# A macaron block with an S4 layer in the middle: the S4 matrix read from DRAM with each partition moved by one value, and the first rows normalized by ScalarE and turned through accumulator banks

## The chip, the core and the metric

The kernel runs on one core of one Trainium2 chip. The metric is the device time of one execution in microseconds (us), taken as the median of several runs. Lower is better. The engines are named as in the profile: PE (TensorE matmul), PEld (its weight loads), DVE (VectorE), ACT (ScalarE), POOL (GpSimd) and SP (SyncE, which issues most DMAs here).

## The reference, cut to what matters

```python
x = L0_attn_u                                   # (2, 1024, 1024) float32
x = x + 0.5 * ffn(layernorm(x))                 # 4-bit weights, HID 1024, INTER 2752
x = x + s4(layernorm(x))
x = x + 0.5 * ffn(layernorm(x))

def ffn(x):                                     # W = scales * (w4 - (z4 + 1)), groups of 128 rows
    return (silu(x @ Wg) * (x @ Wu)) @ Wd

def s4(u):
    Omega = exp(-2j * pi * arange(L) / L)       # L = 1024
    # k00, k01, k10, k11: sums over 64 poles at 1024 points of the circle
    at_roots = c * (k00 - k01 * (1 / (1 + k11)) * k10)
    K = ifft(at_roots, L).real                  # 1024 values, the same for every row
    y = irfft(rfft(u, n=2 * L) * rfft(K, n=2 * L), n=2 * L)[..., :L]
    return y + D[0] * u
```

The last two lines are a causal convolution of each row with K. As a matrix product it needs a Toeplitz matrix: entry (p, c) is K[c - p] for c >= p and 0 before that.

## The kernel before, in words

The 2048 rows are four blocks b of 512 rows (`TB`), each of four tiles t of 128 rows. Eight jobs run in the order `JOBS = [(0, 1), (1, 1), (0, 3), (1, 3), (2, 1), (3, 1), (2, 3), (3, 3)]`: block b and feed-forward k, where k is 1 for the one before S4 and 3 for the one after.

A job has two stages. `gate_up` goes through 64 steps (eight waves of up to three column tiles, times eight row groups of 128). A step loads one weight tile (L456, three steps ahead), multiplies each column tile by the low and the high part of the transposed rows (two PE passes, L496) and then rescales the accumulator in PSUM by the ratio of two groups' scales, on ACT (L472) for the even units and on DVE (L474) for the odd ones. `down` has 44 steps with the same pattern (L555 and again L472 and L474). Job 0 also turns the 4-bit weights into values: DVE subtracts zero points (L395 and L425), SP writes the result to DRAM (`wq`, `wdq`), and all jobs read it from there.

All other work is hung on these steps as hooks (`at(up, step, f)`). The framework then orders the instructions of each engine once, when the program is built; each engine runs its queue in that order and waits on semaphores. So the order on an engine is neither that of the source nor free at run time.

The rows reach PE as follows. `moments` (bn_stats on DVE) and `deviations` (a reciprocal root by three Newton steps, twelve tiny instructions on POOL, L156 to L159) give mean m and reciprocal deviation r. `normalized` (L166) writes (x - m) * r on DVE. `turn` transposes half a tile by four PE transposes into a PSUM bank (L173), ACT copies it as the high part `xTh` (L187), and DVE takes the difference as the low part `xTl` (L188). The banks for this come from the pool `ps` (`bank`), which has two buffers. The accumulators come from the pool `acc`, which has six. For the first block this stands ahead of job 0, the moments in two pairs of tiles, and the dequantization of wave 0 (eight L395) stands between.

The S4 matrix is built once, in the gate_up stage of job 1, by four hooks: `s4_poles` at step 6 (a reciprocal over 128x1024 on DVE, L642), `s4_roots` at step 11, `s4_columns` at step 16 and `s4_toeplitz` at step 22. `s4_roots` takes the sums over poles with eight small matmuls (L681), makes the values at the roots with some 30 DVE instructions of 8 columns, and forms 64 sums of eight products with a table (L727 to L730). `s4_columns` spreads them with 48 DVE instructions of 128x128 (L752 to L754) into the left factors of a product, and `s4_toeplitz` multiplies these with the Fourier tables (16 matmuls of 128x128, two passes each, L764), copies the result on ACT with its columns re-ordered (L771), cuts the lower triangle on POOL (L775) and adds D on the diagonal (L786). The matrix is first read by `convolve` (L797), hung on step 34 of job 1.

Of the kernel before, what the change touches and what calls it, by code (L numbers as in the profile page):

```python
# [9 lines left out]
F32 = mybir.dt.float32  # L10
# [4 lines left out]
AF = mybir.ActivationFunctionType  # L15
ALU = mybir.AluOpType
# [4 lines left out]
P = 128  # L21
# [28 lines left out]
def macaron_s4_kernel(  # L50
# [47 lines left out]
    def bank(name):  # L98
        return ppool.tile([P, 512], F32, tag="ps", name=name)
# [4 lines left out]
    def t4(name):  # L104
        return xpool.tile([P, HID], F32, tag="x", name=name)
# [44 lines left out]
    def deviations(b, k, first=0, eng=None):  # L150

        eng = eng or nc.gpsimd
        mv, ve, r, own = ln.pop((b, first))
        e = small.tile([P, NT], F32, tag="e", name=f"e_{b}_{k}_{first}")[:, own]
        for _ in range(3):
            eng.tensor_tensor(e, r[:, own], r[:, own], ALU.mult)  # L156
            eng.tensor_tensor(e, e, ve, ALU.mult)
            eng.tensor_scalar(e, e, -0.5, 1.5, ALU.mult, ALU.add)
            eng.tensor_tensor(r[:, own], r[:, own], e, ALU.mult)  # L159
        for t in range(own.start, own.stop):  # L160
            ln[b, t] = (mv[:, t, 0:1], r[:, t : t + 1], k)
# [4 lines left out]
        nc.vector.tensor_scalar(n, x[b][t], m, r, ALU.subtract, ALU.mult)  # L166
        return n

    def turned(n, half, name):

        ps = bank(name)
        for k in range(4):
            nc.tensor.transpose(ps[:, bass.ts(k, P)], n[:, bass.ts(4 * half + k, P)], ident)  # L173
        return ps.rearrange("p (c t) -> p c t", c=4)
# [1 line left out]

    pieces = {}

    def turn(b, t, n, half):
        k = ln[b, t][2]  # L180
        if b not in pieces:
            pieces[b] = [
                xtpool.tile([P, NC, TB], F32R, tag="xT", name=f"xT{w}_{b}_{k}") for w in ("h", "l")
            ]
        hi, lo = (a[:, 4 * half : 4 * half + 4, bass.ts(t, P)] for a in pieces[b])
        ps = turned(n, half, f"pt_{b}_{k}_{t}_{half}")
        nc.scalar.copy(hi, ps)  # L187
        nc.vector.tensor_tensor(lo, ps, hi.bitcast(F32), ALU.subtract)  # L188

# [391 lines left out]


    toeplitz = const.tile([P, HID], F32, tag="toeplitz", name="toeplitz")
    s4 = {}

    def s4_poles():
# [88 lines left out]
    def s4_roots():  # L675

        ps = bank("s4_sums")
        for c in range(NC):  # L680
            nc.tensor.matmul(  # L681
                ps[:, 8 * c : 8 * c + 8],
                s4["poles"][:, bass.ts(c, P)],
                s4["weights"],
                start=True,
                stop=True,
            )
        sums = const.tile([P, NC, 8], F32, tag="s4_sums", name="s4_sums_sb")
        nc.vector.tensor_copy(sums.rearrange("p c k -> p (c k)"), ps[:, : 8 * NC])
        half = const.tile([P, 2, NC], F32, tag="s4_half", name="s4_half")  # L690
        nc.sync.dma_start(half, c_half)
        eight = t4("s4_eight").rearrange("p (i n) -> p i n", i=2)
        nc.sync.dma_start(eight, c_eight.partition_broadcast(P))
        hc, hs = half[:, 0, :], half[:, 1, :]

        a = {k: sums[:, :, i] for i, k in enumerate(("00r", "00i", "01r", "01i", "10r", "10i", "11r", "11i"))}
        tmp = {}

        def op(o, l, r, f):
            if o not in tmp:  # L700
                tmp[o] = const.tile([P, NC], F32, tag=f"s4_{o}", name=f"s4_{o}")
            nc.vector.tensor_tensor(tmp[o], l, r, f)
            return tmp[o]

        mul, add, sub = ALU.mult, ALU.add, ALU.subtract
        pr = op("pr", op("m0", a["01r"], a["10r"], mul), op("m1", a["01i"], a["10i"], mul), sub)
        pi = op("pi", op("m0", a["01r"], a["10i"], mul), op("m1", a["01i"], a["10r"], mul), add)
        dr = op("dr", hc, a["11r"], mul)
        nc.vector.tensor_scalar(dr, dr, 1.0, None, add)
        di = op("di", hc, a["11i"], mul)  # L710
        sc = op("sc", op("m0", dr, dr, mul), op("m1", di, di, mul), add)
        nc.vector.reciprocal(sc, sc)
        sc = op("sc", sc, hc, mul)
        nr = op("nr", op("m0", pr, dr, mul), op("m1", pi, di, mul), add)
        ni = op("ni", op("m0", pi, dr, mul), op("m1", pr, di, mul), sub)
        rr = op("qr", a["00r"], op("nr", nr, sc, mul), sub)
        ri = op("qi", a["00i"], op("ni", ni, sc, mul), sub)
        fr = op("fr", op("m0", hc, rr, mul), op("m1", hs, ri, mul), sub)
        fi = op("fi", op("m0", hc, ri, mul), op("m1", hs, rr, mul), add)

        ec, es = (eight[:, i, :].rearrange("p (g c) -> p g c", c=NC) for i in range(2))
        wide = lambda v: v.unsqueeze(1).to_broadcast([P, 64, NC])
        prod = t4("s4_prod").rearrange("p (i n) -> p i n", i=2)
        m0, m1 = (prod[:, i, :].rearrange("p (g c) -> p g c", c=NC) for i in range(2))
        se = const.tile([P, 2, 64], F32, tag="s4_se", name="s4_se")
        for i, (x0, x1, f) in enumerate(((fr, fi, sub), (fi, fr, add))):
            nc.vector.tensor_tensor(m0, ec, wide(x0), mul)  # L727
            nc.vector.tensor_tensor(m1, es, wide(x1), mul)
            nc.vector.tensor_tensor(m0, m0, m1, f)
            nc.vector.tensor_reduce(se[:, i, :], m0, AX.X, add)  # L730
        s4["se"] = se

    def s4_columns():

        cos, sin = t4("s4_tc"), t4("s4_ts")
        nc.sync.dma_start(cos, c_dft[:, 0, :])
        nc.sync.dma_start(sin, c_dft[:, 1, :])
        se = s4["se"]  # L740
        left = [t4("s4_lr"), t4("s4_li")]
        m1 = t4("s4_lm")
        for b in range(8):
            four = lambda ap: ap.rearrange("p (u v) -> p u v", v=8)
            s = [
                se[:, i, 8 * b : 8 * b + 8].unsqueeze(1).to_broadcast([P, 16, 8]) for i in range(2)
            ]
            c, n = four(cos[:, :P]), four(sin[:, :P])
            mb = four(m1[:, bass.ts(b, P)])
            for i, (l0, l1, f) in enumerate(((c, n, ALU.add), (n, c, ALU.subtract))):  # L750
                lb = four(left[i][:, bass.ts(b, P)])
                nc.vector.tensor_tensor(lb, s[0], l0, ALU.mult)  # L752
                nc.vector.tensor_tensor(mb, s[1], l1, ALU.mult)
                nc.vector.tensor_tensor(lb, lb, mb, f)  # L754
        s4["left"], s4["table"] = left, (cos, sin)

    def s4_toeplitz():
        dst = toeplitz.rearrange("p (a b) -> p b a", b=8)
        for i in range(2):
            ps = bank(f"s4_k{i}")  # L760
            for k in range(4):
                b = 4 * i + k
                for part in range(2):
                    nc.tensor.matmul(  # L764
                        ps[:, bass.ts(k, P)],
                        s4["left"][part][:, bass.ts(b, P)],
                        s4["table"][part].rearrange("p (a b) -> p b a", b=8)[:, b, :],
                        start=(part == 0),
                        stop=(part == 1),
                    )  # L770
            nc.scalar.mul(  # L771
                dst[:, 4 * i : 4 * i + 4, :], ps.rearrange("p (b a) -> p b a", b=4), 1.0 / HID
            )
        diag = toeplitz[:, :P]
        nc.gpsimd.affine_select(  # L775
            out=diag,
            in_=diag,
            pattern=[[1, P]],
            compare_op=ALU.is_ge,
            fill=0.0,  # L780
            base=0,
            channel_multiplier=-1,
        )
        d = const.tile([P, 1], F32, tag="s4_d", name="s4_d")
        nc.sync.dma_start(d, dskip.partition_broadcast(P))
        nc.vector.scalar_tensor_tensor(diag, ident, d, diag, ALU.mult, ALU.add)  # L786
        s4.clear()

    def convolve(b, t, lhsT, name):

# [30 lines left out]
    def general():  # L821
# [190 lines left out]

        s4_poles()
        s4_roots()
        s4_columns()
        s4_toeplitz()
        for b in range(TOK // TB):
            load_x(b, rows_of(u, b))
# [16 lines left out]
    def fast():  # L1035
        for j, (b, k) in enumerate(JOBS):
# [50 lines left out]
                at(up, 12, scales_down)  # L1087
                first_weights(up, dn, at)
            if j == 1:
                for s, f in ((6, s4_poles), (11, s4_roots), (16, s4_columns), (22, s4_toeplitz)):  # L1090
                    at(up, s, f)
            if j == 2:
                at(up, 30, in_order)
# [34 lines left out]
    scales(0)  # L1128
    split(0)
    fetch_zeros(0)  # L1130
    for t in (0, 2):
        moments(0, 1, t, 2)
        deviations(0, 1, t)
    for i in range(8):
        dequantize(0, i)
    first = []
    for t in range(NT):
        first.append(normalized(0, t))
        turn(0, t, first[t], 0)
    for t in range(NT):  # L1140
        turn(0, t, first[t], 1)
    x.pop(0)
# [87 lines left out]
```

## Time and profile before

| what | value |
|---|---|
| median of 3 runs | 2228.44 us (2224.03 to 2231.82) |
| the profiled execution's own time | 2229.43 us |
| its span, first to last instruction | 2227.6 us, so 1.8 us lie around it |
| mean granted TensorE clock | 0.989 |
| PE busy | 2146.5 us (96%) |
| DVE busy | 1706.3 us (77%) |
| ACT busy | 1447.6 us (65%) |
| POOL busy | 365.4 us (16%) |
| rescaling on ACT, L472 `pg`, 128x512 | 1264 times 662 ns |
| rescaling on DVE, L474 `pg`, 128x512 | 1144 times 696 ns |

The times of an engine's instructions are from one profiled execution. Matmuls overlap, so the duration of one (some 390 ns for 512 columns) is longer than the step from one to the next, and it is that step that counts in a sum.

### The profile page before, as it was taken

Reading aid. Unit: us, or ns where it says so; the run is one execution under the profiler, and the core shown is the slowest. Engines: PE = TensorE matmul, PEld = TensorE weight load, DVE = VectorE, ACT = ScalarE, POOL = GpSimd, SP = SyncE. Lnnn points to the kernel's source line nnn. Section 1 sums busy time; section 2 is a strip of 40 time slices with the busy share of each in tenths; the row PEclk is TensorE's granted clock in tenths of the full one; section 3 lists DMA queues with packets and bytes.
Section 4 is the critical chain, followed back from the end, with each engine's and each line's share of the span. In section 5 each row is a group of like instructions: output and inputs, shape, how many; then the busy total and the mean of one; then the engine's idle time right before and its main releaser. Section 6 shows DMA issues by size and latency. Waiting matters only on the chain.

```text
span 2227.6 us, 28109 instructions
## 1 busy us (share of the span) xinstructions
PE 2146.5 (96%) x9392; PEld 1690.0 (76%) x9392; DVE 1706.3 (77%) x2705; ACT 1447.6 (65%) x2228; POOL 365.4 (16%) x502
## 2 busy tenths in 40 slices
PE   6998899999999999999999999999999999999998
PEld 4776676767877777888788878777788777888876
DVE  7888779857786878877877777867788677777776
ACT  3777775536764576677767777646776467767775
POOL 1233003212011230122102320102201023012210
PEclk7999999999999999999999999999999999999999
DMA  7888764325443545644455444434444354554444
GB/s 242 284 267 280 251 219 128 121 85 159 135 149 107 174 134 170 225 144 137 143 177 190 130 137 137 148 104 157 138 135 147 107 177 137 153 188 147 134 136 129
DMA packets 161441, 359.86 MB, mean 162 GB/s; under 512 B 20183, under 2 KB 25344, under 8 KB 161290
## 3 DMA queue, kind: packets, MB, share of 16 engines
q1 hardware_dynamic: 160662, 357.64, 50.8%
q8 instruction: 78, 1.28, 0.2%
q14 instruction: 73, 0.60, 0.1%
q10 hardware_dynamic: 628, 0.34, 0.1%
HBM read 307.18 MB, written 50.72 MB: 161 GB/s over the span
## 4 chain that ended last, share of the span: by engine, by line
PE 50%; issue 34%; POOL 7%; DVE 5%; DMA 3%; ACT 0%; SPq 0%; POOLq 0%; DVEq 0%; ACTq 0%
PE pg L496 25%; PE po L555 17%; PE pc L797 5%; POOL hl L523 3%; POOL hh L521 2%; DMA wd<-wdq 1%; DMA w<-wq 1%; DVE pg L474 1%; PE pt L173 1%; PE pb L576 1%; DVE po L474 1%; PE st L173 1%; DVE hf L519 0%; DVE q L395 0%; DMA wdq<-qd 0%
## 5 line engine op out<-in xcount | busy, mean ns | idle before, releaser
L472 ACT ACTIVATE pg<-pg,rat 128x512 f32<-128x512 f32 x1264 | 823.7, 662 | 464.4 <-PE pg L496 461.1
L496 PE MATMUL pg<-xTl,w 128*128 128x512 f32 x2752 | 1088.2, 397 | 33.1 <-DVE pg L474 18.3
L496 PE MATMUL pg<-xTh,w 128*128 128x512 f32 x2752 | 1071.3, 392 | 0.0
L474 DVE TENSOR_TENSOR pg<-pg,rat 128x512 f32<-128x512 f32 x1144 | 780.1, 696 | 168.4 <-PE pg L496 159.6
L496 PEld LDWEIGHTS pg<-xTl,w 128*128 128x128 f32 x2752 | 518.4, 189 | 172.9 <-DVE pg L474 33.5
L496 PEld LDWEIGHTS pg<-xTh,w 128*128 128x128 f32 x2752 | 519.3, 189 | 102.6
L555 PE MATMUL po<-hl,wd 128*128 128x512 f32 x1344 | 538.2, 403 | 14.1 <-DVE po L474 9.2
L472 ACT ACTIVATE po<-po,ratd 128x512 f32<-128x512 f32 x670 | 437.8, 662 | 168.5 <-PE po L555 167.8
L555 PE MATMUL po<-hh,wd 128*128 128x512 f32 x1344 | 521.0, 392 | 0.0
L474 DVE TENSOR_TENSOR po<-po,ratd 128x512 f32<-128x512 f32 x610 | 419.0, 697 | 93.0 <-PE po L555 88.7
L555 PEld LDWEIGHTS po<-hl,wd 128*128 128x128 f32 x1344 | 251.8, 188 | 92.5 <-DVE po L474 21.4
L521 POOL CAST hh<-hf 128x512 fp32r<-128x512 f32 x168 | 109.9, 654 | 1220.1 <-DVE hf L519 1190.2
L555 PEld LDWEIGHTS po<-hh,wd 128*128 128x128 f32 x1344 | 253.3, 188 | 46.2
L523 POOL TENSOR_TENSOR hl<-hf,hh 128x512 fp32r<-128x512 f32 x168 | 221.7, 1320 | 13.3
L519 DVE SCALAR_TENSOR_TENSOR hf<-pg,rat,g 128x512 f32<-128x512 f32 x168 | 125.6, 749 | 80.1 <-ACT g L516 27.9
L516 ACT ACTIVATE g<-pg,rat 128x512 f32<-128x512 f32 x168 | 115.8, 689 | 44.6 <-PE pg L496 41.1
L797 PE MATMUL pc<-toeplitz,st 128*128 128x512 f32 (+3 forms) x384 | 126.5, 486 | 0.0
L797 PEld LDWEIGHTS pc<-toeplitz,st 128*128 128x128 f32 x384 | 70.3, 190 | 57.3 <-issue 46.0
L156 POOL TENSOR_TENSOR e<-r 128x4 f32<-128x4 f32 (+1 forms) x39 | 10.5, 268 | 511.6 <-DVE r L145 509.4
L805 DVE TENSOR_TENSOR x<-x,pc 128x512 f32<-128x512 f32 x32 | 22.0, 687 | 77.6 <-PE pc L797 77.2
L137 DVE BATCH_NORM_STATS2 stats<-x 128x6 f32<-128x512 f32 x96 | 64.6, 680 | 3.2 <-DMA x<-in_L_attn_u_dram 1.9
L187 ACT CAST xTh<-pt 128x512 fp32r<-128x512 f32 x64 | 37.6, 589 | 39.7 <-PE pt L173 39.7
(156 smaller groups left out, 693.0 us busy)
## 6 DMA issues: line engine op xcount, KB each, us to landing
w<-wq SPq DMA_DIRECT2D x320, 384.0 KB
wd<-wdq SPq DMA_DIRECT2D x336, 256.0 KB
w<-wq SPq DMA_DIRECT2D x128, 256.0 KB
w<-wq SPq DMA_DIRECT2D x64, 320.0 KB
x<-in_L_attn_u_dram SPq DMA_DIRECT2D x32, 512.0 KB
wq<-q SPq DMA_DIRECT2D x40, 384.0 KB
wdq<-qd SPq DMA_DIRECT2D x32, 256.0 KB
xs<-x SPq DMA_DIRECT2D x16, 512.0 KB
```

The costliest lines, as they stand in the source:

```text
L137: nc.vector.bn_stats(stats[:, t, i, :], x[b][t][:, bass.ts(i, 512)])
L173: nc.tensor.transpose(ps[:, bass.ts(k, P)], n[:, bass.ts(4 * half + k, P)], ident)
L187: nc.scalar.copy(hi, ps)
L472: nc.scalar.activation(dst, src, AF.Copy, scale=sc)
L474: nc.vector.tensor_tensor(dst, src, sc.to_broadcast([P, TB]), ALU.mult)
L496: nc.tensor.matmul(p, w[:, bass.ts(col, P)], part[:, g, :], start=(g == 0 and k == 0), stop=(g == GK - 1 and k == 1), skip_group_check=True,)
L516: nc.scalar.activation(g, pg, AF.Silu, scale=rat[:, 2 * f, GK - 1 :])
L519: nc.vector.scalar_tensor_tensor(hf, pu, last, g, ALU.mult, ALU.mult)
L521: nc.gpsimd.tensor_copy(hi, hf)
L523: nc.gpsimd.tensor_tensor(lo, hf, hi.bitcast(F32), ALU.subtract)
L555: nc.tensor.matmul(ps[c], w[:, bass.ts(c, P)], part, start=(f == 0 and k == 0), stop=(f == NF - 1), skip_group_check=True,)
L797: nc.tensor.matmul(ps[:, lo - 512 * nh :], lhsT(c), toeplitz[:, lo - P * c : end - P * c], start=(c == 0), stop=(c == last),)
```

## The change: what it does

The change has two parts. In the S4 part, `s4_roots` keeps only 8 of the 64 sums, all its small tiles move into one tile `s4_work`, and a new last DVE instruction turns the sign of the imaginary sums. `s4_columns` is replaced by `s4_response`: 16 matmuls with one moving column each take K from the Fourier tables, DVE scales K and adds D to its first value, and two DMAs write 127 zeros and K to DRAM (`k_dram`). `s4_toeplitz`, now at step 20, reads 128x1024 values back with an access pattern in which each partition starts one value later, and two matmuls with a reversed identity put the partitions in the opposite order. ACT and DVE copy one half each.

In the part for the first rows, the moments of the four tiles are taken together, ACT normalizes in two passes (x - m, then times r), before the dequantization in the source, and the first four halves are turned through the accumulators' pool.

```diff
+    def normalized_on_act(b, t):
+        m, r, k = ln[b, t]
+        n = t4(f"xn_{b}_{k}_{t}")
+        less = small.tile([P, 1], F32, tag=f"less{t}", name=f"less_{t}")
+        nc.gpsimd.tensor_scalar(less, m, -1.0, None, ALU.mult)
+        nc.scalar.activation(n, x[b][t], AF.Identity, bias=less)
+        nc.scalar.activation(n, n, AF.Copy, scale=r)
+        return n
...
-    def turn(b, t, n, half):
+    def turn(b, t, n, half, bank=bank):
...
+    k_dram = dpool.tile([1, P - 1 + HID], F32, tag="k", name="k_dram")
...
-        sums = const.tile([P, NC, 8], F32, tag="s4_sums", name="s4_sums_sb")
+        work = t4("s4_work")
...
-        half = const.tile([P, 2, NC], F32, tag="s4_half", name="s4_half")
+        half = tiny(2 * NC).rearrange("p (i c) -> p i c", i=2)
         nc.sync.dma_start(half, c_half)
...
-        wide = lambda v: v.unsqueeze(1).to_broadcast([P, 64, NC])
+        wide = lambda v: v.unsqueeze(1).to_broadcast([P, 8, NC])
...
+        nc.vector.tensor_scalar(se[:, 1, :], se[:, 1, :], -1.0, None, mul)
         s4["se"] = se
 
-    def s4_columns():
...
-        for b in range(8):
...
-                nc.vector.tensor_tensor(lb, s[0], l0, ALU.mult)
-                nc.vector.tensor_tensor(mb, s[1], l1, ALU.mult)
-                nc.vector.tensor_tensor(lb, lb, mb, f)
+    def s4_response():
+
+        tables = [t4("s4_tc"), t4("s4_ts")]
+        for i in range(2):
+            nc.sync.dma_start(tables[i], c_dft[:, i, :])
+        ps = bank("s4_k")
+        for r in range(8):
+            for i in range(2):
+                nc.tensor.matmul(
+                    ps[:, r : r + 1],
+                    tables[i].rearrange("p (a r) -> p r a", r=8)[:, r, :],
+                    s4["se"][:, i, r : r + 1],
+                    start=(i == 0),
+                    stop=(i == 1),
+                )
+        k = t4("s4_response")
+        d, none = k[:1, 8:9], k[:1, P : 2 * P - 1]
+        nc.sync.dma_start(d, dskip.unsqueeze(0))
+        nc.gpsimd.memset(none, 0.0)
+        nc.vector.tensor_scalar(k[:, :8], ps[:, :8], 1.0 / HID, None, ALU.mult)
+        nc.vector.tensor_tensor(k[:1, 0:1], k[:1, 0:1], d, ALU.add)
+        nc.sync.dma_start(k_dram[:, : P - 1], none)
+        nc.sync.dma_start(k_dram[0, P - 1 :].rearrange("(a r) -> a r", r=8), k[:, :8])
+        s4.clear()
 
     def s4_toeplitz():
...
-        d = const.tile([P, 1], F32, tag="s4_d", name="s4_d")
-        nc.sync.dma_start(d, dskip.partition_broadcast(P))
-        nc.vector.scalar_tensor_tensor(diag, ident, d, diag, ALU.mult, ALU.add)
+        first = k_dram[:]
+        nc.sync.dma_start(rows, bass.AP(first.tensor, first.offset, [[1, P], [1, HID]]))
+        for i in range(NH):
+            ps = bank(f"s4_t{i}")
+            nc.tensor.matmul(ps, turn, rows[:, bass.ts(i, 512)], start=True, stop=True)
+            dst = toeplitz[:, bass.ts(i, 512)]
+            if i:
+                nc.vector.tensor_copy(dst, ps)
+            else:
+                nc.scalar.copy(dst, ps)
...
-                for s, f in ((6, s4_poles), (11, s4_roots), (16, s4_columns), (22, s4_toeplitz)):
+                for s, f in ((6, s4_poles), (11, s4_roots), (16, s4_response), (20, s4_toeplitz)):
...
-    for t in (0, 2):
-        moments(0, 1, t, 2)
-        deviations(0, 1, t)
+    moments(0, 1)
+    deviations(0, 1)
+    first = [normalized_on_act(0, t) for t in range(NT)]
     for i in range(8):
         dequantize(0, i)
-    first = []
     for t in range(NT):
-        first.append(normalized(0, t))
-        turn(0, t, first[t], 0)
+        turn(0, t, first[t], 0, acc)
     for t in range(NT):
         turn(0, t, first[t], 1)
     x.pop(0)
```

## The prediction

> **What bounds the kernel now.** I read the page's busy times first, then its slices.
>
> ```profile
> PE 2146.5 (96%) x9392; PEld 1690.0 (76%) x9392; DVE 1706.3 (77%) x2705; ACT 1447.6 (65%) x2228; POOL 365.4 (16%) x502
> PE   6998899999999999999999999999999999999998
> PEclk7999999999999999999999999999999999999999
> ```
>
> PE bounds it: 81 us of 2227.6 are idle. Only the first slice (55.7 us) shows little PE and a low clock. An engine beside PE can return PE's waits and no more, so the list of PE's waits came next, then the same list for 300 to 460 us, where the S4 matrix is made.
>
> ```profile
> PE pg L496 <- DVE pg L474: 18.3, 22, 3.3
> PE pt L173 <- DVE xn L166: 12.6, 3, 10.4
> ```
>
> ```profile
> PE pg L496 <- DVE pg L474: 1.1, 2, 0.6
> PE pg L496 <- DMA w<-wq: 0.9, 1, 0.9
> ```
>
> (Columns: us in total, times, longest.) The first rows cost PE 12.6 us of waiting before the first product. Around the S4 matrix little is waited for. The timelines of PE, DVE, POOL and SP for the start:
>
> ```profile
> 15.93 0.81 DVE L166 TENSOR_SCALAR xn<-x,mv,r 128x1024 f32<-128x1024 f32 x1 [2.15 <-POOL r L159]
> 17.93 0.94 DVE L395 TENSOR_TENSOR q<-even,z 128x768 fp32r<-128x768 uint8 x1
> 22.46 0.83 POOL L156 TENSOR_TENSOR e<-r 128x2 f32<-128x2 f32 x1 [6.57 <-DVE r L145]
> 29.41 1.54 DVE L166 TENSOR_SCALAR xn<-x,mv,r 128x1024 f32<-128x1024 f32 x2 [1.19 <-POOL r L159]
> ```
>
> POOL's second chain (22.46 to 29.37, twelve steps) sets the third and fourth tile. Its steps take 0.78 to 0.97 us while DVE dequantizes (to 26.95); the last seven take 2.4 us together. Windows of one clock decision, 3.41 us each (columns: window, PE, PEld, DVE, ACT, POOL busy, clock, DMA share, GB/s):
>
> ```profile
> 31.51:34.92 3.41, 3.03 (x12) 2.15 (x12) 2.64 (x6) 1.74 (x3) 0.00 (x0) 0.50 0.81 250
> 34.92:38.33 3.41, 3.41 (x12) 2.63 (x11) 2.82 (x4) 0.90 (x2) 0.00 (x0) 0.50 0.87 317
> 38.33:41.74 3.41, 3.41 (x23) 2.73 (x22) 2.91 (x6) 3.11 (x6) 0.00 (x0) 1.00 0.70 251
> ```
>
> PE runs at half clock from 11 us, and gets full clock only after a window without a gap (34.92 to 38.33).
>
> **The first rows, part by part.** Two small S4 loads that stood before the x loads on SP go, so x comes 0.9 us earlier (x loads start at 2.67 before). DVE loses four L166 (0.82 each, 3.3 us) and two waits for POOL (2.15, 1.19); the dequantization starts at about 16.4 instead of 17.93, when its zero points land (17.2 before, 0.9 earlier too). Before, DVE's seed of the second r was done at 22.39, which is 4.46 after the first L395; now one seed for all four tiles comes at 20.9, DVE's last L395 ends at 25.4 (before 26.90), and POOL's only chain ends at about 27.4 instead of 29.37. ACT then does four second passes (times r). No row shows ACT on 128x1024 here; the nearest, L472, is 662 ns for 512 columns, so a pass lies between 0.66 and 1.32 us. I take 1.0, nearer the upper end since the columns double. The rows are ready at 28.4, 29.4, 30.4 and 31.4; the first passes (x - m) are done while POOL works.
>
> PE waits for the first rows until 28.4, as before (28.37), then turns eight halves (1.09 us each at half clock). All eight groups stand ahead of the first product in PE's order; before, two stood behind it. The last two use the two banks of `ps` and wait for the low parts of the halves before them: ACT's first copy of a second half ends near 34.6, DVE's low parts (0.69 each) at 35.3 and 36.3. So the first L496 starts at 36.9 to 37.5 instead of 35.04. Against this, it starts at full clock, as PE turns from 28.4 to 35 without a gap, and has no turns between its products (0.71 and 0.32 us of extra step, L173 at 36.92 and 38.20). Its weights are there: the dequantization is 1.5 us earlier, the first weight landed at 35.00 before, and now about 33.5. The fourteenth product stood at 41.23, with 0.6 of a scale turn before it that is moved; mine comes at 36.9 to 37.5 plus 13 times 0.227, or 39.9 to 40.5. Even, then, or a little earlier; but DVE's low parts and the two L395 of wave 1 end at 40.4 to 41.4 against 40.21, and the first rescaling waits for them. I take +0.7, between -1.6 (POOL's chain without the slow steps) and +4 (next sentences).
>
> The gaps decide the clock. The row: 0.38 us of idle in 31.51 to 34.92 (3.03 busy of 3.41), and the next window stayed at 0.50. If the new order has such a gap in the last window before the first product, the products of the next one run at half clock, which costs 1.7 us for a window, 3.4 for two. The nearest row on whether turns count at all is the warm-up, 32 turns and nothing else:
>
> ```profile
> 0.79:4.20 3.41, 2.67 (x13) 2.67 (x14) 0.00 (x0) 0.00 (x0) 0.64 (x4) 1.00 0.31 31
> 4.20:7.61 3.41, 3.41 (x18) 3.41 (x17) 2.87 (x12) 0.00 (x0) 0.00 (x0) 1.00 0.84 285
> 7.61:11.03 3.42, 0.58 (x5) 0.34 (x3) 1.48 (x4) 0.96 (x1) 0.00 (x0) 1.00 0.90 291
> ```
>
> From 0.205 us for a turn (2.67 / 13) the step falls to 0.116 (0.58 / 5) after a full window of turns alone, so I let turns count.
>
> The Trainium skill, "TensorE: Matmul & The Clock Gate", section "Part 4: PE-mode transpose", says that the clock gate does not engage for transposes, as they do not count as PE-busy in the same way. By that rule the first products would start at half clock and the start would come to +2.4 or more; the warm-up's rows speak against it.
>
> **The S4 matrix, part by part.** DVE loses 48 instructions of 128x128 (a step of 0.20 each, 9.7 us) and most of the sums of products (about 6.5 of eleven instructions of 512 columns, 0.6 each), some 16 us. That relief lies beside PE. PE's idle between 380 and 405 is all it could return:
>
> ```profile
> 381.43 0.50 PE L496 MATMUL pg<-xTl,w 128*128 128x512 f32 x1 [0.28 <-DVE hf L519]
> 383.73 0.50 PE L496 MATMUL pg<-xTl,w 128*128 128x512 f32 x1 [0.64 <-DVE pg L474]
> 389.35 0.62 PE L764 MATMUL s_k<-s_tc,s_lr 128*128 128x128 f32 x2
> 402.93 0.70 PE L496 MATMUL pg<-xTl,w 128*128 128x512 f32 x2 [0.85 <-DMA w<-wq]
> ```
>
> That is 1.77 us; I take 1.5 back. What is late after the first two is the weights' DMA, which is the third and need not go.
>
> On PE, 32 passes (L764, 128 columns) cost 7.5 us: 11.4 us from 389.35 to 400.8, less 17 products of 0.227. The 32 that replace them have one column. If the weight load sets their step, it stays 0.226 (7.4 us); the 16 small L681 (8 columns) step by 0.213 at half clock, 0.11 at full, which gives 3.4. I take the middle, 5.2. The two products with the reversed identity add four passes of 512 fp32 columns at 0.429, 1.7 us. So PE's own work changes by 5.2 + 1.7 - 7.5 = -0.6.
>
> The new wait is the round trip through DRAM. The two products stand in PE's order some 30 products (6.8 us) behind the last one-column product. Before they can start: DVE scales K and adds D, behind one rescaling (1.0 us together); the write lands (the first `wq` write landed 2.3 us after its issue, so 2.3); and the read of 512 KB comes back. Its nearest row is a table of the same size, read by all partitions from one row:
>
> ```profile
> 315.79 0.42 SPq L611 DMA_DIRECT2D s_cos<-in_c_rows_dram  x1
> 321.94 0.75 DVE L633 TENSOR_SCALAR s_dr<-s_cos,s_vc 128x1024 f32<-128x1024 f32 x1 [0.82 <-DMA s_cos<-in_c_rows_dram]
> ```
>
> That is 6.1 us; an x load took 3.6. I take 5.0. So 1.0 + 2.3 + 5.0 = 8.3 (7 to 10), and PE stands 1.5 us (0 to 3). Behind the waiting product stand all further products; behind the waiting read on SP stands one weight load, three steps ahead of its use, which a few us of delay can make late too: +1.0 (0 to 3). ACT's and DVE's copies of the result stand behind PE, and `convolve` reads the matrix only at 440, some 35 us later, so these are covered; POOL's two memsets and the lost triangle and diagonal are off the path. S4 sum: -1.5 - 0.6 + 1.5 + 1.0 = +0.4, between -4.2 (7.5 - 3.4 - 1.7 and 1.8 saved, nothing new) and +7.8 (the first rival).
>
> **Sum.** +0.7 + 0.4 = +1.1 on the profiled execution's 2229.43, 2230.5; that execution lies 1.0 above the median (2228.44), so 2229.5.
>
> **The rivals.** A difference of 0.3% (6.7 us) is about what a measurement of this kernel can tell from no change; the shown runs spread by 7.8.
>
> Slower: the rows land late. The read's rows overlap and start at any multiple of 4 bytes, which no row shows. From a trip of 6.8 us on, each further us is PE's idle; at 12 us it is 5.2. A window with that much idle halves the clock: after the 3.3 us of waiting at 511.5 the window 516.2 to 519.6 ran at half, worth 1.7. With the delayed weight load (3) and -2.1 saved, S4 gives +7.8, and with +0.7 from the start the median goes to 2237. For: every piece is new and serial. Against: 30 products stand in front. Chance 0.34.
>
> Faster: POOL's steps run at 0.3 us since DVE's seed and waits lie otherwise, the rows come 2 us earlier (start -1.6); the one-column products step by 0.11 (-4.1 + 1.7), the trip is covered, all 1.8 us of waits return, and the half clock seen at 352 to 362 is gone (-2.5): -8.3, or 2220. For: each has a row. Against: the last belongs to the poles' reciprocal, which is kept. Chance 0.27.
>
> Third: job 0 swallows the start's difference, since its later waits for weights (seven, 7.3 us from 40 to 300) end by DMA whatever the start does; then +0.4 remains, 2228.8, inside the forecast.
>
> **How the numbers follow.** Forecast, no change: 0.39, its own range 2223 to 2235. Both sides are near, as the sums' ends (-5.8 and +11.8) are wider than the bound. 2219 to 2239 leaves out 1 in 10 at each end. Faster 0.27, same 0.39, slower 0.34.
>
> **What would show it.** Right: first L496 at 36.9 to 37.5 with the clock at 1.00; PE waiting 1 to 3 us for the read of K's rows near 400; no idle by DVE near 381 to 384. Wrong: first product at half clock or after 39; a wait for the rows above 5 us; ACT passes over 1.3 us; one-column products slower than 0.23 each; a changed wait in the jobs after 460 us.

## The result, and the profile after

The changed kernel took 2232.14 us in the median (2230.6 to 2234.3), the kernel before 2230.13 (2224.03 to 2232.68; the three runs told above and one more). The ratio is 1.0014 with a 95% interval of 0.999 to 1.0038: no difference that the measurement can tell. The profiled execution took 2234.30 us, span 2232.5, which is 4.9 us more than the one of before.

The page's busy times and slices:

```profile
PE 2152.1 (96%) x9396; PEld 1696.8 (76%) x9396; DVE 1693.7 (76%) x2653; ACT 1455.9 (65%) x2235; POOL 361.5 (16%) x496
PE   5998999999999999999999999999999999999998
PEclk7999998999999999999999999999999999999999
```

DVE lost 12.6 us of work and PE gained 5.6 us of busy time with only four more instructions. One slice more has its clock under 9 tenths, the seventh (335 to 391 us). The waits of PE (us in total, times, longest):

```profile
PE pg L505 <- DVE pg L483: 16.3, 21, 3.3
PE pt L182 <- ACT xn L175: 14.1, 1, 14.1
PE pt L182 <- DVE xTl L197: 2.0, 1, 2.0
```

PE now waits for ACT instead of DVE at the start (14.1 us in all, 12.6 before), and has a new wait for the low parts. The timelines of POOL, ACT, DVE and PE at the start:

```profile
26.33 0.20 POOL L159 TENSOR_TENSOR r<-r,e 128x4 f32<-128x4 f32 x1
26.56 4.27 ACT L175 ACTIVATE xn<-xn,r 128x1024 f32<-128x1024 f32 x4 [7.71 <-POOL r L159]
30.74 2.02 ACT L196 CAST xTh<-pt 128x512 fp32r<-128x512 f32 x4
31.33 3.68 DVE L197 TENSOR_TENSOR xTl<-pt,xTh 128x512 fp32r<-128x512 f32 x6 [6.83 <-ACT xTh L196]
34.47 1.72 PE L182 MATMUL pt<-ident,xn 128*128 128x128 f32 x8 [1.97 <-DVE xTl L197]
35.83 0.78 PE L505 MATMUL pg<-xTl,w 128*128 128x512 f32 x1
```

ACT's four second passes stand in front of its first copy (30.74), though PE began to turn at 27.76. DVE has nothing to do for 6.83 us. Then two banks hold PE up for 1.97 us, and the first product comes at 35.83. The windows (columns as above: window, PE, PEld, DVE, ACT, POOL, clock, DMA share, GB/s) show what the gap does:

```profile
28.09:31.51 3.42, 3.42 (x17) 2.90 (x16) 0.18 (x1) 3.42 (x5) 0.00 (x0) 0.50 0.75 246
31.51:34.92 3.41, 1.44 (x13) 1.16 (x11) 3.41 (x6) 2.22 (x5) 0.00 (x0) 1.00 0.92 327
34.92:38.33 3.41, 3.41 (x12) 2.79 (x11) 3.21 (x7) 2.24 (x4) 0.00 (x0) 0.50 0.14 51
```

A window of turns without a gap is followed by full clock. The window with the gap (1.44 us busy) is followed by half clock, and the first five products run in it.

In the S4 stage, the one-column products (thirty passes in a row from 388.68 to 395.64, two stand ahead at 385.07), then the products with the reversed identity, on PE's timeline; then SP's:

```profile
388.98 0.61 PE L760 MATMUL s_k<-s_work,s_tc 128*128 128x1 f32 x2
395.17 0.61 PE L760 MATMUL s_k<-s_work,s_ts 128*128 128x1 f32 x2
404.64 1.88 PE L795 MATMUL s_t<-s_rows,s_turn 128*128 128x512 f32 x4
```

```profile
396.66 0.32 SPq L774 DMA_DIRECT2D k_dram<-s_response  x1
399.43 0.37 SPq L792 DMA_DIRECT2D s_rows<-k_dram  x1
```

The rows of K landed at 403.32 by their semaphores, so nobody waits for the trip. The cost is elsewhere, in the windows:

```profile
386.47:389.88 3.41, 3.16 (x15) 2.63 (x13) 2.56 (x7) 1.32 (x2) 0.00 (x0) 1.00 0.33 115
389.88:393.30 3.42, 3.42 (x16) 3.42 (x16) 0.00 (x0) 0.00 (x0) 0.00 (x0) 1.00 0.12 47
393.30:396.71 3.41, 3.41 (x14) 3.22 (x15) 0.82 (x3) 0.26 (x1) 0.00 (x0) 0.50 0.00 0
396.71:400.12 3.41, 3.41 (x10) 2.63 (x9) 1.40 (x2) 1.32 (x3) 0.00 (x0) 0.50 0.10 17
```

PE is busy without a gap from 389.88 on, and yet the clock falls to half for two windows. Ten large products (512 columns) run in 4.41 us (395.64 to 400.05) instead of 2.28.

To see where the 4.9 us came from, I took the start of the same product in both traces (passes with gate_up weights, L505 or L496, counted from 0). Product 0 is 0.79 us later, product 700 (324 us) 0.99, the first product of `convolve` (440 us) 3.64, the last shown of `down` (2203 us) 3.88. Some 1 us more lies at the very end. So in this pair job 0 changed little, the S4 stage cost 2.65 us, and after it the two executions run in step.

### The profile page after: what moved, and what is told of

Its sections match the earlier page's. It is cut to its first block, busy times and chain, and to the rows that moved or that the text cites. A ratio compares the mean times of both kernels' runs of the same rounds, so it can differ in the third digit from the quotient of the medians.

```text
span 2232.5 us, 28079 instructions
## 1 busy us (share of the span) xinstructions
PE 2152.1 (96%) x9396; PEld 1696.8 (76%) x9396; DVE 1693.7 (76%) x2653; ACT 1455.9 (65%) x2235; POOL 361.5 (16%) x496
## 3 DMA queue, kind: packets, MB, share of 16 engines
q8 instruction: 78, 1.28, 0.2%
## 4 chain that ended last, share of the span: by engine, by line
PE 53%; issue 31%; POOL 6%; DVE 5%; DMA 3%; ACT 0%; SPq 0%; POOLq 0%; DVEq 0%; ACTq 0%
PE pg L505 28%; PE po L564 18%; PE pc L810 5%; POOL hl L532 3%; POOL hh L530 2%; DVE pg L483 1%; DMA w<-wq 1%; DMA wd<-wdq 1%; PE pt L182 1%; PE pb L585 1%; DVE po L483 1%; PE st L182 1%; DMA wdq<-qd 0%; DVE q L404 0%; DVE hf L528 0%
## 5 line engine op out<-in xcount | busy, mean ns | idle before, releaser
L505 PE MATMUL pg<-xTl,w 128*128 128x512 f32 x2752 | 1092.5, 398 | 27.0 <-DVE pg L483 16.3
L505 PE MATMUL pg<-xTh,w 128*128 128x512 f32 x2752 | 1077.6, 393 | 0.0
L505 PEld LDWEIGHTS pg<-xTl,w 128*128 128x128 f32 x2752 | 521.6, 190 | 163.9 <-DVE pg L483 29.7
L505 PEld LDWEIGHTS pg<-xTh,w 128*128 128x128 f32 x2752 | 522.2, 190 | 104.8 <-issue 0.2
L156 POOL TENSOR_TENSOR e<-r 128x4 f32<-128x4 f32 x36 | 9.7, 268 | 498.6 <-DVE r L145 496.6
L182 PE MATMUL pt<-ident,xn 128*128 128x128 f32 x256 | 42.6, 285 | 16.0 <-ACT xn L175 14.1
```

The source lines that it names most:

```text
L505: nc.tensor.matmul(p, w[:, bass.ts(col, P)], part[:, g, :], start=(g == 0 and k == 0), stop=(g == GK - 1 and k == 1), skip_group_check=True,)
```

## The experiments

Three readings of the traces carry the comparisons, since the times alone can't show 2 us: the start of the first product, the stage from product 700 to `convolve`'s first product, and the part of that stage from product 820 on. Product 820 stands behind a half clock near 351 us that all kernels have, and ahead of the changed S4 products, so the last reading holds the least chance: kernels that differ only in their start agree in it to 0.3 us. Job 0 (product 0 to 700) is left out; it took 282.6 to 290.3 us in the thirteen traces, with no order by kernel.

| kernel | first product, us | S4 stage, us | from product 820, us | half clock near 389 to 402 | ratio to before, 95% interval |
|---|---|---|---|---|---|
| before | 35.05 | 116.42 | 75.64 | no | 1 |
| changed | 35.83 | 119.07 | 77.16 | two windows | 1.0014 (0.999 to 1.0038) |
| S4 part alone | 35.18 | 118.27 | 76.92 | two | 1.0003 (0.9992 to 1.0014) |
| first rows alone | 36.66 | 116.97 | 75.60 | no | 0.9998 (0.9988 to 1.0008) |
| 64 equal columns | 35.19 | 119.40 | 77.29 | two | 1.001 (0.9999 to 1.002) |
| spread | 35.72 | 116.46 | 74.56 | no | 1.0001 (0.9991 to 1.001) |
| normalized by DVE | 33.77 | 118.87 | 77.08 | two | 0.999 (0.9979 to 1.0002) |
| six in accumulators | 34.49 | 118.28 | 76.90 | two | 1.0002 (0.9991 to 1.0012) |
| 128 equal columns | 35.38 | 115.76 | 75.04 | no | 0.9993 (0.9982 to 1.0004) |
| late start | 41.20 | 118.74 | 77.14 | two | 1.0013 (1.0002 to 1.0024) |
| DVE and 128 columns | 33.08 | 117.20 | 75.03 | no | 0.9987 (0.9977 to 0.9997) |
| old start, 128 columns | 35.73 | 115.68 | 75.02 | no | 1.0 (0.9989 to 1.0012) |
| DVE, 128 columns, sums too | 33.60 | 117.08 | 77.26 (other order) | no | 0.9985 (0.9976 to 0.9994) |

My theory was that the small products (few columns each) count as idle for the clock. The rivals were the trip through DRAM and the start.

**The two parts alone.** The S4 part with the start of before:

```diff
-    moments(0, 1)
-    deviations(0, 1)
-    first = [normalized_on_act(0, t) for t in range(NT)]
+    for t in (0, 2):
+        moments(0, 1, t, 2)
+        deviations(0, 1, t)
...
-        turn(0, t, first[t], 0, acc)
+        first.append(normalized(0, t))
+        turn(0, t, first[t], 0)
```

> The S4 part alone; the first rows are normalized and turned as before. Theory (the small products count as idle for the clock): the first product stands near 35 us as before; 16 one-column products in a row near 390 to 396 us, then one to two 3.41 us windows at 0.50 though PE is busy in every one of them; convolve's first product comes 1.7 to 2.6 us later than before, counted from the same product near 324 us. Rival (the trip through DRAM is what costs): a wait of PE for the rows of K of over 1 us. Rival (the start-up causes the whole 3.8 us of after): the lag at convolve is under 1 us. Median 0 to 4 us over before.

The stage grew by 1.85 us against before (1.28 of it from product 820 on), with the two half-clock windows and no wait for the rows. The loss is the S4 part's own. The other part alone is the kernel before with the changed start:

> The first rows' part alone; the S4 matrix is made as before. Theory: the first product stands at 35.5 to 36.2 us after a wait of about 2 us for the low parts (two banks) and runs at half clock for its first 2.4 us; what is left of the start at 324 us lies between -1 and +1.5 us, as job 0 has waits of its own; no half clock between 389 and 400 us. One more window at half clock near 362 us if the lag at 324 us is near 1 us. Rival (the start is the whole of the 3.8 us): lag of over 2.5 us at convolve. Median -1 to +3 us against before.

No half clock from 389 to 400, 0.55 us in the stage, and nothing from product 820 on. The first product came at 36.66, later than expected and at full clock where I expected half, and 4.6 us of lead at product 700 were outside my band: job 0 took 282.6 us here, the shortest of all. The rival that the start is the whole loss falls. That job 0 can differ by so much hides anything that the start gives or takes.

**64 equal columns.**

```diff
-                    ps[:, r : r + 1],
+                    ps[:, 64 * r : 64 * r + 64],
...
-                    s4["se"][:, i, r : r + 1],
+                    s4["se"][:, i, r : r + 1].to_broadcast([P, 64]),
...
```

> The changed kernel, but each one-column product takes its column 64 times (a broadcast operand) and the first of the 64 results is used: the same weight loads, the same order. Theory (the clock counts how long the array streams columns, not how long PE is busy): the clock stays at 1.00 from 389 to 400 us, the ten products at 0.43 us step by 0.23 again (-2.1 us), and the rows of K now come 0.5 to 1.5 us late, since they have 30 products of 0.227 as cover, 6.8 us, and landed 7.7 us after the last small product; net lag of 1 to 1.6 us less than in the changed kernel. Rival (weight loads set the clock, or any product under 128 columns counts as idle): the half clock stays and the lag is the same as in the changed kernel. Rival (64 columns cost more time than one): the step of the small products rises above 0.238 us by the same share.

The half clock stayed, so this expectation failed. The windows, the first of them filled with these products:

```profile
387.81:391.22 3.41, 3.41 (x16) 3.41 (x16) 0.00 (x0) 0.00 (x0) 0.00 (x0) 1.00 0.03 9
391.22:394.64 3.42, 3.42 (x13) 3.23 (x14) 0.32 (x2) 0.48 (x1) 0.00 (x0) 0.50 0.00 0
```

The step of 0.2375 us (0.475 for a pair of passes) was that of one column, and in the changed kernel it is the same before and after the clock is halved. So the columns are free here. What is left to set the step is the weight load: PEld is busy in all of the first window. What the clock takes as idle reaches to 64 columns at least.

**Spread.** One product pair in each of eight steps, and the read at step 30:

```diff
...
+                for i in range(8):
+                    at(up, 19 + i, lambda i=i: s4_response(i))
```

> The changed kernel, but the one-column products stand in eight hooks (steps 19 to 26, two products each with 12 products of 512 columns between) and the rows are read at step 30. Theory: in each 3.41 us window most of the time is streamed, so the clock stays at 1.00; the ten products at half clock are gone (-2.1 us) and no wait for the rows takes their place, since the read has more than 8 us of cover; the lag at convolve falls by about 2 us against the changed kernel, unless a switch between small and large products costs more than 0.1 us each (16 switches). Rival (a window needs to be wholly free of small products, as one of 1 us of idle was enough at the start): every window from 389 to 412 us runs at half clock, +5 us or more.

The clock stayed at 1.00 and the stage fell by 2.6 us against the changed kernel, to that of before; from product 820 on it is 1.1 us shorter than before. A window need not be free of small products to keep the full clock. With 12 large passes between two small groups, most of each window belongs to large ones.

**128 equal columns**, in two banks:

```diff
-                    ps[:, r : r + 1],
+                    pair[r // 4][:, bass.ts(r % 4, P)],
...
-                    s4["se"][:, i, r : r + 1],
+                    s4["se"][:, i, r : r + 1].to_broadcast([P, P]),
...
```

> As the run with 64 equal columns, but with 128, in two banks. There, 64 columns kept the half clock. Theory (a window is taken as idle where the array streams less than some share of the time; 512 columns in two passes take 0.455 us, so 128 take 0.057 of a step of 0.238, 24%, and 64 take 12%): if the share needed is under 24%, the clock stays at 1.00 behind the small products and the lag over the S4 stage falls by 2 us; if it is over 24%, half clock again from one window behind the first full window of small products, with the same lag of 2.6 to 3.0 us from 324 us to convolve. I expect the half clock, since at the start windows with four products of 512 columns in 3.41 us (27%) were followed by half clock. Rival (the number of columns of a product counts, and the turns with their 128 columns raised the clock): full clock.

The other way round than I expected: the clock stayed full, behind a window as full of small products as before.

```profile
388.69:392.11 3.42, 3.42 (x16) 3.42 (x17) 0.31 (x2) 0.00 (x0) 0.00 (x0) 1.00 0.01 2
392.11:395.52 3.41, 3.41 (x17) 2.79 (x16) 2.52 (x5) 1.99 (x3) 0.00 (x0) 1.00 0.07 8
```

The same small products with the same weights stand in a row, and PE is as busy; what differs from the two runs with half clock is the columns, and the second bank that they need. That is what shows the theory, and every trace agrees: in the four with 128 columns (this one and the last three below) a window full of these products kept the full clock, in the six with one or 64 columns in a row it was followed by half. The point lies between 64 and 128 columns at this step; where, and whether it is a share of time or something else, stays open. The trip is also shown to be covered without the half clock: the first large product behind the row started at 392.00, the rows landed at 398.67, and the products that read them started at 398.92 with no wait.

**The start.** The half clock at the first product of the changed kernel was chance. Four other traces have the same start (first rows alone, 64 equal columns, spread, 128 equal columns). In them the gap before the last two turns was 1.13 to 1.18 us instead of 1.97, and the first product ran at full clock, at 35.19 to 36.66 us. The windows with 128 equal columns:

```profile
30.30:33.71 3.41, 2.94 (x14) 2.45 (x12) 2.48 (x5) 3.28 (x7) 0.00 (x0) 0.50 0.92 268
33.71:37.13 3.42, 2.76 (x16) 2.29 (x17) 3.39 (x8) 2.21 (x5) 0.00 (x0) 1.00 0.59 226
```

Further on, the changed start is ahead of the old one: product 96 starts at 61.49 to 64.08 us in these five traces and at 64.93 to 65.34 in the three with the old start. At product 700 the two ranges overlap (319.30 to 324.88 and 321.96 to 325.49).

ACT's normalization undone, the rest of the start kept:

```diff
-    first = [normalized_on_act(0, t) for t in range(NT)]
...
+        first.append(normalized(0, t))
         turn(0, t, first[t], 0, acc)
```

> The changed kernel, but the first rows are normalized by DVE in one pass, as before, right ahead of each turn; the moments of four together and the turns through the accumulators stay. Theory (ACT's queue is what delays the start: its four second passes, 1.07 us each, stand ahead of its copies of the high parts, while DVE idles 6.8 us): PE's first turn at 27.0 to 27.6 us, the first copy of a high part right behind it at about 28.7 instead of 30.74, and the first product at 32.7 to 34.5 instead of 35.83, unless its weights are later. Rival (two banks are what delays it): first product within 0.5 us of 35.8. The median moves by less than a measurement tells, -2 to +1 us.

The timelines of DVE, PE and ACT:

```profile
26.57 2.98 DVE L166 TENSOR_SCALAR xn<-x,mv,r 128x1024 f32<-128x1024 f32 x4 [2.06 <-POOL r L159]
28.59 0.59 ACT L196 CAST xTh<-pt 128x512 fp32r<-128x512 f32 x1 [17.04 <-PE pt L182]
33.77 0.48 PE L505 MATMUL pg<-xTl,w 128*128 128x512 f32 x1
```

DVE, which is idle there, does the four in 2.98 us against ACT's 4.27, ACT copies from 28.59 on, and the first product is 2.06 us earlier, at full clock. One group of turns now stands behind the first product, which is a part of that; but product 96 too is early, at 59.50 to 60.20 us in the three traces with this start, against 61.49 at best with ACT. The bank for the last two turns alone:

```diff
-        turn(0, t, first[t], 1)
+        turn(0, t, first[t], 1, bank if t < 2 else acc)
```

> The changed kernel, but the last two of the second halves too are turned through accumulators. Theory: PE's wait of 1.1 to 2.0 us for the low parts before the last two turns goes, PE turns without a gap up to the first product, which starts at 34.0 to 35.0 us at full clock. Rival (ACT's copies and DVE's low parts follow each other at 0.65 us each and end when they end): the first product, which needs all low parts of the first half only, starts earlier, but PE then waits as long in the first twelve products. The median moves by -2 to +1 us.

The first product came 1.34 us earlier, but PE then waited 0.50 and 0.97 us for DVE among the next products. Product 24 was at 41.78 and product 96 at 62.30; the five traces with two banks have them at 40.76 to 42.56 and 61.49 to 64.08. So no lead can be seen there any more, as the rival says. And a start made late by 64 more turns:

```diff
+    ps = acc("late")
+    for _ in range(64):
+        nc.tensor.transpose(ps[:, :P], first[3][:, 7 * P :], ident)
```

> The changed kernel with 64 more turns of 128 columns on PE ahead of the first product, into an accumulator that nobody reads: the first product is late by some 6 to 13 us (to be read in the trace). Theory (job 0 is paced by the weights that DVE and the DMAs prepare, so it gives back a late start in part): the lag at 324 us is less than half of the lag of the first product, within the 4 us by which job 0 differs from run to run; the median rises by 0 to 6 us. Rival (PE bounds job 0, a late start counts in full): the median rises by the whole delay.

The first product was 5.4 us later than in the changed kernel, product 96 2.1 us, product 700 2.5 us, and the ratios agree (1.0013 against 1.0014). But against the five traces with the same start the delays are 4.5 to 6.0, 2.1 to 4.7 and 2.5 to 8.0 us, and the interval of the late run alone reaches from 0.4 to 5.4 us over before. So it is not shown how much of a late start job 0 gives back.

**Both mends.** DVE normalizes and the small products have 128 columns:

> The two mends of the changed kernel together: DVE normalizes the first rows in one pass (as in the run that undid ACT's passes alone), and the small products take their column 128 times. Theory: first product at 33.5 to 34.5 us, no half clock from 389 to 400 us, 115.5 to 116.5 us from the product at 324 us to convolve's first (119.07 in the changed kernel). The median is 1 to 4 us below the kernel before; job 0 gives most of the earlier start back, so that 2 us of it are the S4 stage. Rival (the stage's gain is given back at the next wait): convolve 2 us earlier, but the same end.

2227.01 us in the median (2223.84 to 2228.87), ratio 0.9987 (0.9977 to 0.9997). By the interval this version is faster than before, by some 2.9 us. The stage missed my band (117.20), by the clock near 350 us, which the end of this section takes up; from product 820 on it takes 75.03 us against 77.16 in the changed kernel. With the old start instead:

> The S4 part alone (first rows as before) with the small products' column taken 128 times. Theory: from 324 us to convolve 115.5 to 116.5 us against 116.42 before and 118.27 in the S4 part alone with one column; no half clock from 389 to 400 us; median 0 to 2 us below the S4 part alone, so from 1 us below to 1 us above the kernel before. Rival (the new start is needed for it): no change against the S4 part alone.

115.68 us in the stage, 0.7 under before, as expected, and a time that can't be told from before.

**The sums over the poles with 128 columns:**

```diff
-                s4["weights"],
+                s4["weights"].unsqueeze(1).to_broadcast([P, 16, 8]),
...
```

> As the run with both mends, and the eight products over the poles (8 columns, sixteen passes near 356 us, also in the kernel before) take their columns 16 times, 128 in all. Theory (products of 8 columns hold the clock down as those of one did): the half clock that begins near 351 us with the stall of PE ends after two windows (6.8 us) instead of three or four (10.2 or 13.7); the stage from 324 us to convolve takes 113.5 to 115.5 us. Rival (the clock is held down by the stall alone): three or four windows as before.

Three windows, not two, and 117.08 us in the stage, so the expectation failed. The order also changed: the sums no longer stand in one row but among large products, from 350 to 361 us, and PE waits again near 376 us. Its windows still say something:

```profile
352.26:355.67 3.41, 3.41 (x13) 2.93 (x12) 1.29 (x2) 1.32 (x2) 2.47 (x4) 0.50 0.00 0
355.67:359.09 3.42, 3.42 (x18) 2.84 (x17) 3.08 (x5) 0.77 (x2) 0.00 (x0) 1.00 0.55 163
```

1.69 us of the first window belong to the sums with 128 columns, and full clock follows.

The other twelve traces have the sums with 8 columns, sixteen passes in one row of 3.1 us, and a window's edge cuts this row elsewhere in each execution. The half clock near 351 us lasts three windows in before, in 128 equal columns and in old start with 128 columns; there products 800 to 900 take 30.31 to 30.38 us. It lasts four windows in nine others, where they take 30.56 to 31.92. What tells the two apart is how much of the row the third or fourth window holds: with 0.20 to 0.43 us of it full clock followed, with 0.58 us or more half clock, though PE is busy in all of the window. Here is the case with 0.58, in the run with both mends:

```profile
354.56:357.97 3.41, 3.41 (x10) 2.40 (x11) 0.00 (x0) 1.32 (x2) 2.22 (x5) 0.50 0.00 0
357.97:361.38 3.41, 3.41 (x10) 2.64 (x8) 2.02 (x3) 0.19 (x1) 0.00 (x0) 0.50 0.35 115
```

So the small products of the kernel before cost a window too, or not, by chance. In the pair of before and changed this is 1.1 of the 2.65 us, all of it between products 810 and 820 (363 to 367 us); the change itself costs the 1.5 us from product 820 on.

## Why the prediction was right, point by point

The time was inside the range and "no change" was the forecast. Of the sum behind it, +1.1 us, several steps were wrong, and it is luck that they stayed small: the S4 part missed its term by 1 to 2 us and the start went the other way, but both lie below what the medians of this kernel can tell.

- **First product at 36.9 to 37.5, at full clock.** 35.83 in half clock in the changed kernel's profile, 35.19 to 36.66 at full clock in the four other traces with this start. DVE's seed was done at 19.98 and not at 20.9, POOL's chain ended at 26.53 and not 27.4, and the turns began 0.6 us earlier. They also took less than 1.09 us a half as soon as the clock was full. The gap before the last two, which I had named but not put into the clock, took the clock away in the changed kernel's profile alone.
- **The start's term, +0.7.** Wrong in sign as far as it can be followed, though the first product of the profiled pair is 0.79 us late. The fourteenth product was at 40.06 (39.9 to 40.5 predicted, 41.23 before), and the delay that was to come behind it did not: DVE's first rescaling began at 39.18, against 40.13 before. Product 96 was early in all five traces; what is left of it at the end of job 0 can't be told.
- **The gaps decide the clock.** Not so. A gap of 0.38 us in a window of twelve turns was followed by half clock before, and gaps of 0.47 to 0.53 us in windows of fourteen turns by full clock in three runs (2.94 us busy, above). In the S4 stage half clock came without any gap.
- **Turns count for the clock.** Shown, by the window 28.09 to 31.51 of turns alone and the full clock behind it. The warm-up says the same more clearly than the prediction read it: from start to start a turn takes 0.213 us and then 0.109. The rule of the Trainium skill, "TensorE: Matmul & The Clock Gate", section "Part 4: PE-mode transpose", doesn't hold for these turns; whether they run in the mode that the page means, the trace doesn't tell.
- **ACT's passes at 1.0 us.** 1.05 from one to the next. Right, but ACT's copies stand behind all four passes, and the prediction did not price that: up to 2.06 us of the first product.
- **One-column products, 5.2 us.** The term that was mis-sized: 32 steps of 0.2375, 7.6 us, above the upper end of 7.4. The lower end rested on 0.11 us for a small pass at full clock, which no run shows: the step is 0.2375 at both clocks, and the sums' 0.204 (0.213 in the prediction) was seen at half clock alone.
- **Half clock behind them.** The step that was missing: +2.1 us. The profile of before held the row for it. The sixteen passes of 8 columns all but fill one window, and the next stays at half although PE has no gap:

```profile
355.77:359.18 3.41, 3.41 (x17) 3.41 (x17) 2.56 (x4) 0.66 (x1) 3.33 (x4) 0.50 0.03 5
359.18:362.59 3.41, 3.41 (x8) 2.35 (x9) 0.00 (x0) 1.32 (x2) 1.27 (x1) 0.50 0.00 0
```

  I had put this half clock down to the stall before it.
- **Two reversed products, 1.7 us.** 1.7 (404.64 to 405.96, and 0.4 of a long step behind). Right.
- **The trip, 8.3 us, and a wait of 1.5.** 7.7 us from the end of the small products to the landed rows, and no wait: the half clock stretched the 30 passes of cover to 9.0 us. In the three runs with 128 columns and the sums as before the trip was 6.4 to 6.7 us under 6.9 of cover. No trace shows PE waiting for the rows, but in the late run they landed only 0.14 us ahead of their use. The rival "rows land late" is out, but only just.
- **A weight load late by 1.0.** It was issued at 402.34 behind the read and landed at 405.18; nobody waited.
- **1.5 us of waits back.** 1.35: the waits of 0.28, 0.64 and 0.85 gave way to 0.25 and 0.17.
- **S4 sum +0.4.** +1.5 from product 820 on, 1.3 to 1.7 in all runs with one or 64 columns in a row; over the whole stage, with the chance near 351 us, +2.65 in the profiled pair and 1.85 to 2.98 in the others. Without the half clock (128 columns) the sum is -0.6. DVE's work in the stage fell by 11.7 us (104.76 to 93.11), not 16; PE's idle from product 820 on fell from 2.42 to 0.84. The measured terms (7.6 + 1.7 - 7.5 for the products, 2.1 for the clock, -1.6 for the idle) make +2.3; the 0.8 us between this and +1.5 no reading here explains.
- **Job 0 swallows the start.** Neither shown nor refuted: its run-to-run spread of 7.7 us is larger than any start term.

## What to carry to other kernels

Relief of an engine that PE does not wait for is worth about PE's waits and not the engine's work; here PE lost 1.6 us of idle, and at most 0.8 us beside, for 11.7 us less work on DVE. When a step is cut down to products with few columns, put them among large ones, or widen them (here to 128 columns) if their step does not depend on the columns: here a row of small ones longer than a clock window cost the next two windows half their speed. Work moved to another engine's queue must be priced by what stands behind it there. A change of under 0.2% is judged by the same instruction in the traces, and in several traces of each kernel: the place of a clock window alone moved single ones by 1 us.

## What the runs showed of the hardware

- The granted clock does not follow PE's busy time. Windows of 3.41 us busy out of 3.41 were followed by half clock when filled with products of 1 or 64 columns, stayed at half when they held 0.58 us or more of products of 8 columns, and were followed by full clock with 128 columns.
- The clock changed only at edges 3.41 us apart, which lay elsewhere in each execution, and took two rates, 1.00 and 0.50. The Trainium skill, "TensorE: Matmul & The Clock Gate", section "Part 1: The HAM clock gate (the "warmup" mystery)", says the same of the window (free-running, 3413 ns) and the two rates, and that a monitor sets the clock by how busy PE has been. By these runs "busy" can't be read as PE's busy time in the profile: the number of columns counts too.
- A pass's step did not depend on its columns: 0.2375 us with 1, 64 and 128 in a row of products with different weights. Nor did it change when the clock was halved.
- Writing K to DRAM landed 1.4 to 3.4 us from its issue in eleven traces, and reading 128 rows that start 4 bytes apart 3.7 to 5.0, between the two rows that bounded the read (3.6 and 6.1).
